# A hand-made instruction planner learns which work of VectorE and GpSimd to keep apart, the query tokens are put in order at their split, and the gates of the last token pair move forward

## The chip, the cores and the metric

The kernel runs on one core of one Trainium2 chip. The metric is the device time of one launch in microseconds. The runs of the kernel before gave 760.32, 760.10 and 758.83 us, median 760.1.

Five engines work side by side, each through its own queue in order: TensorE (PE; its weight loads are shown as PEld), VectorE (DVE), ScalarE (ACT), GpSimd (POOL) and SyncE (SP, which only issues DMAs). An instruction starts when those before it on its engine have been issued and the semaphores it waits for are set.

## The reference, cut to what matters

One pre-norm transformer block over 2 x 1024 tokens of width 1024 in float32:

```python
x = x + attn(layernorm(x))     # conv of width 3 (1024 -> 768), split in q, k, v of 256
                               # 16 heads of 64, causal softmax inside blocks of 128 tokens
                               # output product (1024 -> 256), then projection (256 -> 1024)
x = x + ffn(layernorm(x))      # y = x @ W_base.T + b_base
                               # + sum over 4 experts of alpha_e * 2 * (x @ A_e.T) @ B_e.T
                               # alpha = softmax(log(prior) + router logits of the 4 experts)
```

## The kernel before, in words

**Numbers.** Nearly every product is made of three float32r matmuls: each operand is split in a rounded part ("hi", a copy on ScalarE) and the rest ("lo", a subtraction on VectorE), and hi x hi, hi x lo and lo x hi are summed (`three`, L141). So each operand costs one ScalarE and one VectorE instruction.

**Three parts.** (1) To about 230 us: layernorm, transposes and the convolution, which is done with 6 products of transformed tokens and weights instead of 12; its results `m` go to DRAM. (2) About 230 to 520 us: attention. (3) From there: projection, second layernorm, and the feed-forward product by Strassen's scheme: for each pair `m` of 128-token groups, 7 products of 4x4 blocks take the place of 8. Sums of token blocks (S1 to S4) are made on the way; sums of weight blocks (T1 to T4, `plan_differences`) are made on GpSimd during attention (`stage_add`, L1080), split, and stored to DRAM (`wsd`).

**Attention.** 32 steps `i` (4 chunks of 512 tokens x 8 pairs of heads) are planned two at a time, 16 "pairs" `K`. For each step there are query and key products (`query_key`, out through ScalarE at L897), scores (`scores`, L905), mask (`masked`, VectorE, L920, reads PSUM), row maximum (`maximum`, VectorE, L929), exponentials with sums (`exponentials`, ScalarE, L934), reciprocal (`reciprocal`, VectorE, L941), the division (`normalized`, GpSimd, L945), transposes (L952) with copies out (`transposed_p`: half on VectorE at L960, half on ScalarE at L962), the product with the values (`attend`, L969), its split (L983, L990), and the output product (`out_proj`). Values are made for four heads at a time (`values`), and copied out by VectorE where `b` is odd (L871) and by ScalarE where it is even (L873).

**Tokens.** For the next chunk, the convolution's six results are loaded and joined on VectorE, all from SBUF: `tokens_join` in three parts (L560 and L561; L571, L572 and L573; L575 and L577), then split by `tokens_hi` (ScalarE, L585) and `tokens_lo` (VectorE, L590). Tiles 0 and 1 of a chunk feed the queries, 2 and 3 the keys, 4 and 5 the values. Tokens lie in the order (block, residue mod 4, position); the queries are brought into the order (block, position, residue) when they leave PSUM, by a strided write at L897.

**The planner.** The program's order isn't the source's order. Every piece of work is an `Op` with an engine, an assumed duration (`takes`), a due time, the earliest lead before it, the Ops it comes after with a `lag`, and places (buffers, PSUM banks) that it needs and gives. `trace()` plays the engines against each other in assumed time: again and again it takes, among all engines, the Op that can start earliest, preferring on each engine the first by due time that doesn't leave it idle. Then it emits all Ops sorted by their planned start. So assumed durations, lags and due times set nothing but the order in the queues; on the chip the semaphores of the data decide when a thing starts.

```python
t = [a.end + a.lag for a in self.after]
...
t = max(free.get(e, 0.0), o.due - o.lead + late, t)
```

**The last token pair.** In the loop over `m`, the small products for the gates (`z_products`, `plan_zs`), their turn (`z_turn`, in `plan_gate`), the gate's softmax (`gate_logits`, `gate_exp`, `gate`), a transpose (`transpose_z`, `plan_z`) and the four expert matmuls (`experts`, `plan_e`) come after product 5, 7 or 3 of the pair. In the pairs before the last, the next pair's projection and transposes lie between them. Each expert matmul adds into the PSUM bank of one quarter of the output (`py_a`, `py_e`, `py_f`, `py_c`), `add_y` (VectorE, L1376) adds that to the residual, and `store` writes it out, by halves in the last pair.

Of the kernel before, what the change touches and what calls it, by code (L numbers as in the profile page):

```python
# [21 lines left out]
P = 128  # L22
# [17 lines left out]
def preln_block_kernel(  # L40
# [229 lines left out]
    class Op:  # L270
        def __init__(self, engine, takes, due, lead, after, f, lag=0.15, need=(), give=()):
            self.engine, self.takes, self.due, self.lead = engine, takes, due, lead
            self.after, self.f, self.lag = [o for o in after if o is not None], f, lag
            self.need, self.give = need, give
            self.start = self.end = None
            plan.append(self)

        def earliest(self):
# [3 lines left out]
            t = [a.end + a.lag for a in self.after]  # L282
# [7 lines left out]
    def trace():  # L290
# [4 lines left out]
        while any(todo.values()):  # L295
            best = None
            for e, ops in todo.items():
                held = None
                for o in ops:
# [3 lines left out]
                    t = max(free.get(e, 0.0), o.due - o.lead + late, t)  # L303
                    if held is None or t < held[0]:
                        held = (t, o)
# [6 lines left out]
            free[o.engine] = o.end  # L312
            for k in o.need:
                places[k].remove(min(places[k]))
# [268 lines left out]
    def tokens_hi(ch, c):  # L583
        yt = t4(f"yt_{ch}_{c}", (2, TC))
        nc.scalar.copy(yt[:, 0], ys[ch, c])  # L585
        ys[ch, c] = ys[ch, c], yt

    def tokens_lo(ch, c):
        y, yt = ys[ch, c]
        nc.vector.tensor_tensor(yt[:, 1], y, yt[:, 0], ALU.subtract)  # L590
# [276 lines left out]
    def values_out(G, b):  # L867
        if G not in vhs:
            vhs[G] = ap_.tile([P, NB, 512], F32, tag="vh", name=f"vh_{G}")
        if b % 2:  # L870
# [17 lines left out]
    def query_key_out(i, q):  # L888
# [3 lines left out]
        out, pq = qk, pqs.pop((i, q))  # L892
        if q == 0:

            out = qk.rearrange("p (b j r) -> p b r j", b=NB, r=4)
            pq = pq.rearrange("p (b r j) -> p b r j", b=NB, r=4)
        nc.scalar.activation(out, pq, AF.Identity, bias=b_ap[:, hp : hp + 1], scale=sc)  # L897
# [374 lines left out]
    def z_products(m):  # L1272
# [13 lines left out]
        for o in ("A11", "A12", "S1"):  # L1286
            opd.pop((m, o))
# [101 lines left out]
    MM = 1.37  # L1389
    NI = NCHUNK * NHP  # L1390
# [13 lines left out]
    def op(key, e, takes, due, after, f, lead=14.0, **kw):  # L1404
        d[key] = Op(e, takes, due, lead, [d[a] for a in after if a in d], f, **kw)
        return d[key]

    def plan_q(i):
        ch, hp = divmod(i, NHP)
        for q in range(2):  # L1410
            pe(("Q", i, q), MM, [("y", ch, 2 * q), ("y", ch, 2 * q + 1)], partial(query_key, i, q),
               give=("t4",) * 2 if hp == NHP - 1 else ())
            op(("q", i, q), ACT, 0.55, at[0], [("Q", i, q)], partial(query_key_out, i, q),
               need=("t2",), give=("m",))

    def plan_v(G, b):
# [3 lines left out]
        op(("v", G, b), *((DVE, 0.6) if b % 2 else (ACT, 0.55)), at[0], [("V", G, b), ("v", G, 0)],  # L1420
           partial(values_out, G, b), need=("vh",) if b == 0 else (), give=("m",))

    def plan_s(i):
        pe(("S", i), 1.0, [("q", i, 0), ("q", i, 1)], partial(scores, i), need=("m",) * 2,
           give=("t2",) * 2)

    def plan_softmax(i, due):
        for j in range(2):
            op(("k", i, j), DVE, 0.69, min(due - 11.0, d["S", i].due + 4.0) + 0.7 * j, [("S", i), ("k", i, j - 1)],
               partial(masked, i, j), need=("a4",) if j == 0 else (), give=("m",), lead=40.0)  # L1430
        op(("x", i), DVE, 1.21, due - 9.5, [("k", i, 0), ("k", i, 1)], partial(maximum, i),
           lead=40.0)
        for j in range(2):
            op(("e", i, j), ACT, 1.6, due - 8.0 + 1.6 * j, [("x", i)], partial(exponentials, i, j),
               lead=40.0)
        op(("r", i), DVE, 0.2, due - 4.0, [("e", i, 0), ("e", i, 1)], partial(reciprocal, i),
           lead=40.0)
        op(("n", i), POOL, 2.3, due - 3.7, [("r", i)], partial(normalized, i), lead=40.0)

    def plan_t(i):  # L1440
        plan_softmax(i, at[0])
        for j in range(2):
            pe(("T", i, j), 0.44, [("n", i)], partial(transpose_p, i, j),
               give=("a4",) if j == 1 else ())
            op(("t", i, j), *((DVE, 0.65) if j == 0 else (ACT, 0.55)), at[0], [("T", i, j)],
               partial(transposed_p, i, j), need=("a4",) if j == 0 else (), give=("m",))

    def plan_o(i):
        pe(("O", i), 0.9, [("t", i, 0), ("t", i, 1)] + [("v", i // 4, b) for b in range(NB)],
           partial(attend, i), give=("a4",) + (("vh",) if i % 4 == 3 else ()))  # L1450
        op(("h", i), ACT, 0.6, at[0] + 1.0, [("O", i)], partial(attended_hi, i), need=("a4",))
        op(("l", i), DVE, 0.7, at[0] + 2.0, [("h", i)], partial(attended_lo, i), give=("m",))

    def plan_w(i):
# [3 lines left out]
        if hp == NHP - 1:  # L1458
            for wc in range(NWC):
                op(("oh", ch, wc), ACT, 0.7, at[0] + 1.0, [("W", i)], partial(out_hi, ch, wc),  # L1460
                   need=("t4",))
                op(("ol", ch, wc), DVE, 0.75, at[0] + 2.0, [("oh", ch, wc)],
# [5 lines left out]
    def plan_tokens(ch, c, due):  # L1468
# [3 lines left out]
        op(("yj", *k), DVE, 0.75, due - 5.0, [("yd", *k)], partial(tokens_join, ch, c, 0),  # L1472
           need=("t2", "t2"))
        op(("yk", *k), DVE, 1.0, due - 4.0, [("yj", *k)], partial(tokens_join, ch, c, 1))
        op(("yl", *k), DVE, 0.95, due - 3.0, [("yk", *k)], partial(tokens_join, ch, c, 2),
           give=("ml", "t2"))
        op(("yh", *k), ACT, 0.6, due - 1.8, [("yl", *k)], partial(tokens_hi, ch, c),
           need=("t4",))
        op(("y", *k), DVE, 0.64, due - 0.8, [("yh", *k)], partial(tokens_lo, ch, c),
           give=("t2",))  # L1480

    def plan_raw(k, src, due, hi, lo, pools, after=(), lead=8.0):
# [4 lines left out]
        op(("rh", *k), ACT, 0.58, due - 1.5, [("rd", *k), *after], partial(hi, *k[1:]), lead=lead)  # L1487
        op(("rl", *k), DVE, 0.66, due - 0.7, [("rh", *k)], partial(lo, *k[1:]), lead=lead,
           give=(pool,))

    def plan_x(n, due):
# [5 lines left out]
        op(("xb", n), POOL, 2.4, due - 4.0, [("X", n), ("pb",)], partial(add_projb, g))  # L1497

    def plan_p(n):
# [9 lines left out]
        for h in range(2):  # L1509
# [3 lines left out]
            op(("r", n, h, 0), DVE, 0.68, at[0] + 0.5, [("P", n, h), ("xb", n)],  # L1513
               partial(residual, g, h), give=("m",))
        op(("xs", n), DVE, 1.65, at[0] + 2.0, [("r", n, 0, 0), ("r", n, 1, 0)], partial(x_stats, g))
# [3 lines left out]
    def plan_tx(m, t, h):  # L1519
# [9 lines left out]
        if o == "A21":  # L1529
            more(("c", o), ACT, 0.6, 0.5, [("A", o)], partial(keep_a21, m), need=("a4",), give=("m",))  # L1530
        else:
            more(("h", o), ACT, 0.6, 0.5, [("A", o)], partial(op_hi, m, o), need=("a4",))
# [348 lines left out]
```

## Time and profile before

| what | us |
|---|---|
| profiled execution, device time | 760.05 |
| its span, first to last instruction | 758.3 |
| PE busy / idle in the span | 744.3 / 14.0 |
| DVE busy | 604.3 |
| ACT busy | 422.0 |
| POOL busy | 213.0 |
| `normalized` (L945), 32 times | 64.8 |
| queries out (L897, `bq`), 32 times | 38.0 |
| granted clock of TensorE (share) | 0.998 |

In a timeline, each line has the start and the duration in us, the engine, the line of the kernel, the operation, the tiles written and read, shapes, and how many were merged (x6). In brackets stands how long the engine was idle before it, and what ended that. A table of windows gives, for each stretch, its length and the busy time of PE, PEld, DVE, ACT and POOL with instruction counts, then TensorE's granted clock, the DMA engines' share and GB/s. Matmuls are pipelined: the durations of those that follow each other overlap a little, so the pace is read from the starts.

### The profile page before, as it was taken

How to read it: one execution, taken by the hardware profiler on the slowest of the kernel's cores; microseconds unless marked ns; L12 is line 12 of the kernel's file. 1: busy time of each engine (PE TensorE's matmuls, PEld its weight loads, DVE VectorE, ACT ScalarE, POOL GpSimd, SP SyncE). 2: the span in 40 equal slices, each digit the busy share in tenths (PEclk: the TensorE clock that was granted, in tenths of full speed). 3: DMA queues.
4: the chain of work that ended last, by engine and by line, in shares of the span. 5: the costliest groups of instructions: out<-in, count | busy, mean ns of one | idle time of the engine just before them, and what ended most of it. 6: DMA issues, size and time to landing. Idle time of an engine off the chain costs nothing.

```text
span 758.3 us, 12914 instructions
## 1 busy us (share of the span) xinstructions
PE 744.3 (98%) x4740; PEld 634.7 (84%) x4740; DVE 604.3 (80%) x1050; ACT 422.0 (56%) x1028; POOL 213.0 (28%) x170
## 2 busy tenths in 40 slices
PE   8999999999999999899999999999999999999997
PEld 8999988888888878787878888888888888888885
DVE  7888899889766899999899988789666767567652
ACT  6887336455736978797687989763212212212120
POOL 3224321210002224334332313362332241322410
PEclk9999999999999999999999999999999999999999
DMA  9937994994852323253316554795645565465552
GB/s 341 374 104 210 251 263 110 291 286 103 275 149 90 106 77 112 104 196 132 105 56 209 189 167 153 271 411 216 245 177 222 217 271 207 193 246 220 201 228 105
DMA packets 65279, 149.46 MB, mean 197 GB/s; under 512 B 5902, under 2 KB 24734, under 8 KB 60096
## 3 DMA queue, kind: packets, MB, share of 16 engines
q1 hardware_dynamic: 61488, 138.64, 50.6%
q0 software_dynamic: 3728, 10.00, 7.2%
q8 instruction: 37, 0.61, 0.3%
q14 instruction: 26, 0.21, 0.1%
HBM read 114.01 MB, written 34.60 MB: 196 GB/s over the span
## 4 chain that ended last, share of the span: by engine, by line
PE 82%; DVE 9%; ACT 6%; DMA 1%; issue 1%; SPq 0%; DVEq 0%; ACTq 0%
PE pm L141 26%; PE pq L141 8%; PE py_e L1262 6%; PE pp L141 6%; PE py_a L1262 6%; PE py_c L1262 6%; PE pw L141 4%; PE pv L141 4%; ACT p L934 3%; PE py_b L1262 3%; PE po L969 3%; PE pt L952 2%; PE s L905 2%; PE pz L1279 2%; PE trx L1202 2%; PE tr L386 1%
## 5 line engine op out<-in xcount | busy, mean ns | idle before, releaser
L141 PE MATMUL pm<-v,u 128*128 128x256 f32 (+1 forms) x1152 | 203.3, 337 | 1.1 <-ACT v L474 0.6
L141 PEld LDWEIGHTS pm<-v,u 128*128 128x128 f32 x1152 | 177.7, 190 | 24.3 <-ACT v L474 0.9
L934 ACT ACTIVATE p<-p,nmx 128x128 f32<-128x128 f32 x256 | 99.6, 397 | 12.8 <-DVE nmx L929 12.8
L945 POOL TENSOR_TENSOR p<-p,rs 128x1024 f32<-128x1024 f32 x32 | 64.8, 2025 | 144.8 <-DVE rs L941 120.3
L141 PE MATMUL pq<-yt,wqk 128*128 128x512 f32 x384 | 93.2, 397 | 0.0
L141 PEld LDWEIGHTS pq<-yt,wqk 128*128 128x128 f32 x384 | 70.7, 188 | 17.3 <-issue 1.9
L1165 POOL TENSOR_TENSOR xr<-xr,projb 128x1024 f32<-128x1024 f32 x16 | 38.3, 2398 | 96.7 <-DMA xr<-in_x 79.7
L934 ACT ACTIVATION_READ_ACCUMULATOR p<-p,nmx 128x1 f32 x256 | 50.1, 196 | 0.0
L920 DVE TENSOR_TENSOR p<-s,mask 128x512 f32<-128x512 f32 x64 | 42.2, 680 | 7.8 <-PE s L905 7.6
L141 PE MATMUL pw<-oT,wot 128*128 128x512 f32 x192 | 48.2, 398 | 0.0
L141 PE MATMUL pv<-wvt,yt 128*128 128x512 f32 x192 | 47.1, 395 | 0.0
L897 ACT ACTIVATE qk<-pq,bq 128x512 f32<-128x512 f32 x32 | 38.0, 1187 | 11.0 <-PE pq L141 8.2
L141 PEld LDWEIGHTS pv<-wvt,yt 128*128 128x128 f32 x192 | 36.0, 187 | 8.7
L141 PEld LDWEIGHTS pw<-oT,wot 128*128 128x128 f32 x192 | 35.9, 188 | 8.8 <-DVE oT L990 0.3
L424 POOL DMA_DIRECT2D g<-in_conv_w x24 | 21.2, 925 | 68.4 <-ACT g L420 36.6
L1240 ACT CAST S<-s 128x512 fp32r<-128x512 f32 x32 | 19.7, 621 | 35.8 <-DVE s L1234 31.5
L446 DVE TENSOR_TENSOR u<-g,u 128x768 fp32r<-128x768 f32 x40 | 37.5, 951 | 1.5 <-ACT u L442 1.4
L929 DVE TENSOR_REDUCE nmx<-p 128x8 f32<-128x1024 f32 x32 | 38.3, 1201 | 0.0
L905 PE MATMUL s<-qk,qk 64*128 64x128 f32 x512 | 34.6, 280 | 3.1 <-ACT vh L873 2.5
L905 PEld LDWEIGHTS s<-qk,qk 64*128 64x128 f32 x512 | 30.9, 187 | 7.6 <-ACT vh L873 3.2
L442 ACT CAST u<-g 128x768 fp32r<-128x768 f32 x40 | 32.5, 837 | 4.8 <-PE pm L141 4.7
L1360 ACT COPY u<-py_a 128x512 f32<-128x512 f32 x8 | 4.7, 588 | 53.0 <-PE py_a L1262 53.0
(204 smaller groups left out, 1539.9 us busy)
## 6 DMA issues: line engine op xcount, KB each, us to landing
wb_B<-wsd_B SPq DMA_DIRECT2D x32, 1024.0 KB, 4.8
g<-in_conv_w SPq DMA_DIRECT2D x48, 384.0 KB, 7.7
mdr<-m SPq DMA_DIRECT2D x36, 256.0 KB, 2.9
g<-in_conv_w POOLq DMA_DIRECT2D x24, 384.0 KB, 7.4
xt<-in_x SPq DMA_DIRECT2D x16, 512.0 KB, 9.5
xr<-in_x SPq DMA_DIRECT2D x16, 512.0 KB, 4.5
out<-xr SPq DMA_DIRECT2D x14, 512.0 KB, 2.9
ml<-mdr SPq DMA_DIRECT2D x18, 384.0 KB, 3.9
```

The costliest lines, as they stand in the source:

```text
L141: nc.tensor.matmul(ps, l[a], r[b], start=first and i == 0, stop=last and i == 2)
L442: nc.scalar.copy(us[v, dc][0], raws[v, dc])
L446: nc.vector.tensor_tensor(lo, raws.pop((v, dc)), hi, ALU.subtract)
L897: nc.scalar.activation(out, pq, AF.Identity, bias=b_ap[:, hp : hp + 1], scale=sc)
L905: nc.tensor.matmul(s[j][:, b, :], qh[ts(j, DH), ts(b, P)], kh[ts(j, DH), ts(b, P)], start=True, stop=True,)
L920: nc.vector.tensor_tensor(ps[i][0][:, ts(j, NB), :], ss[i][j], mask[:, None, :].to_broadcast([P, NB, P]), ALU.add,)
L929: nc.vector.tensor_reduce(nmx, p, AX.X, ALU.max, negate=True)
L934: nc.scalar.activation(p[:, k, :], p[:, k, :], AF.Exp, bias=nmx[:, k : k + 1], accum_out=sm[:, k : k + 1],)
L945: nc.gpsimd.tensor_tensor(p, p, rs[:, :, None].to_broadcast([P, 2 * NB, P]), ALU.mult)
L969: nc.tensor.matmul(po[ts(j, DH), ts(b, P)], vh[:, b, ds((i % 4) * P + j * DH, DH)], pT[:, j, ts(b, P)], start=True, stop=True,)
L1165: nc.gpsimd.tensor_tensor(xrs[g], xrs[g], pwt["b"], ALU.add)
L1262: nc.tensor.matmul(pys[m, b], l[x], r[y], start=opens and c == 0 and i == 0, stop=c == NH - 1 and i == 2, skip_group_check=not opens,)
```

## The change

It has five parts.

1. **The planner knows a port.** An Op may have `port=True`. Such an Op starts in the plan no earlier than the end of the last such Op on any engine. It is set for GpSimd's tensor work (`normalized`, `add_projb`, `stage_add`, `add_u`) and for VectorE's instructions with two tensor inputs in SBUF (`tokens_join`, `tokens_lo`, the "lo" of weights, stages and S sums, `za_lo`, `zd_lo`, `finish_bb`). It isn't set where an input is in PSUM, nor for `maximum`, `x_stats` and `x_norm`. This acts in the plan alone: no wait is added to the program.
2. **Assumed times.** Most `takes` are changed, by 0.03 to 0.4 us (`normalized` 2.3 to 1.9, masks 0.69 to 0.6, maximum 1.21 to 1.12). The default lag after VectorE and ScalarE goes from 0.15 to 0.25, between two Ops of TensorE to 0.
3. **Tokens and values.** The queries' tokens are written in their final order by `tokens_hi` and `tokens_lo` (tiles 0 and 1), and the strided write at L897 goes. `vh` is copied by VectorE for `b == 1` only.
4. **Stage work moves.** The differences start at the pairs 2, 4, 6, 8 instead of 1, 4, 6, 9 and have later due times within a pair; the splits of B11, B21 and B22 are spread over the pairs 10 to 14 instead of 11 to 14. Token tile 5 is planned ahead of others.
5. **The last pair** has its own order: gate products after product 1, gate in product 6, experts behind products 2, 3 and in the middle of 4, with stores of quarters between; the last expert matmul is ahead of the second half of product 4, and only its addition is left behind.

The diff, cut to its core (the many changed durations are left out):

```diff
-        def __init__(self, engine, takes, due, lead, after, f, lag=0.15, need=(), give=()):
+        def __init__(self, engine, takes, due, lead, after, f, lag=0.15, need=(), give=(), port=False):
...
+            self.port = port
...
-            t = [a.end + a.lag for a in self.after]
+            t = [a.end + (a.lag if a.engine != self.engine or a.engine != "PE" else 0.0)
+                 for a in self.after]
...
+                    if o.port:
+                        t = max(t, free.get("port", 0.0))
...
+            if o.port:
+                free["port"] = o.end
...
     def tokens_hi(ch, c):
         yt = t4(f"yt_{ch}_{c}", (2, TC))
-        nc.scalar.copy(yt[:, 0], ys[ch, c])
+        y, hi = ys[ch, c], yt[:, 0]
+        if c < NWC:
+
+            y = y.rearrange("p (b r j) -> p b r j", b=NB, r=4)
+            hi = hi.rearrange("p (b j r) -> p b r j", b=NB, r=4)
+        nc.scalar.copy(hi, y)
         ys[ch, c] = ys[ch, c], yt
...
-        nc.vector.tensor_tensor(yt[:, 1], y, yt[:, 0], ALU.subtract)
+        lo, hi = yt[:, 1], yt[:, 0]
+        if c < NWC:
+            y = y.rearrange("p (b r j) -> p b j r", b=NB, r=4)
+            lo, hi = (t.rearrange("p (b j r) -> p b j r", b=NB, r=4) for t in (lo, hi))
+        nc.vector.tensor_tensor(lo, y, hi, ALU.subtract)
...
-        if b % 2:
+        if b == 1:
             nc.vector.tensor_copy(vhs[G][:, b, :], pvs.pop((G, b)))
...
-        out, pq = qk, pqs.pop((i, q))
-        if q == 0:
-
-            out = qk.rearrange("p (b j r) -> p b r j", b=NB, r=4)
-            pq = pq.rearrange("p (b r j) -> p b r j", b=NB, r=4)
-        nc.scalar.activation(out, pq, AF.Identity, bias=b_ap[:, hp : hp + 1], scale=sc)
+        pq = pqs.pop((i, q))
+        nc.scalar.activation(qk, pq, AF.Identity, bias=b_ap[:, hp : hp + 1], scale=sc)
...
+        if e in (DVE, ACT):
+            kw.setdefault("lag", LAG)
...
-        op(("n", i), POOL, 2.3, due - 3.7, [("r", i)], partial(normalized, i), lead=40.0)
+        op(("n", i), POOL, 1.9, due - 3.7, [("r", i)], partial(normalized, i), lead=40.0, lag=0.3,
+           port=True)
...
-    DIFFERENCES = (1, 4, 6, 9)
+    DIFFERENCES = (2, 4, 6, 8)
     todo = [(n, c) for n in ("B11", "B21", "B22") for c in range(NH)]
-    SPLITS = {K: todo[3 * i : 3 * i + 3] for i, K in enumerate((11, 12, 13, 14))}
+    SPLITS = {10: todo[:2], 11: todo[2:5], 12: todo[5:7], 13: todo[7:10], 14: todo[10:]}
...
+    m = NM - 1
+    plan_product(m, 1)
+    plan_zs(m)
+    plan_product(m, 6, [partial(plan_gate, m)])
+    stream(m, "B21")
+    plan_product(m, 2)
+    plan_z(m)
+    plan_e(m, 0, 0, "a", [("Y", m, 2, 1)])
+    plan_store(m, 0, 0)
+    plan_product(m, 5)
+    stream(m, "B22")
+    plan_product(m, 7)
+    plan_product(m, 3)
+    plan_e(m, 0, 1, "e", [("Y", m, 3, 1)])
+    plan_store(m, 0, 1)
+    plan_e(m, 1, 1, "f", [], True)
+    plan_store(m, 1, 1)
+    plan_product(m, 4, [partial(plan_e, m, 1, 0, "c", [("Y", m, 4, 0)], sum_up=False)])
+    plan_add(m, 1, 0, "c", [("Y", m, 4, 1)])
+    plan_store(m, 1, 0)
```

## The prediction

> **What bounds the kernel now.** I read the page's busy shares first.
>
> ```profile
> PE 744.3 (98%) x4740; PEld 634.7 (84%) x4740; DVE 604.3 (80%) x1050; ACT 422.0 (56%) x1028; POOL 213.0 (28%) x170
> ```
>
> TensorE is busy 98% of the span and the change takes no matmul away. So the question is only where TensorE waits or lags, and which part of that can go. I looked at three stretches.
>
> (1) The timeline of PE in the attention part. One pair of head steps is always 24 `pq`, 12 `pw`, 12 `pv`, 16 `pt`, 32 `s` and 32 `po` matmuls, so the distance between the first `po` of one pair and of another measures the pace.
>
> ```profile
> 260.42 1.97 PE L969 MATMUL po<-pT,vh 128*64 128x128 f32 x32
> ...
> 437.69 1.97 PE L969 MATMUL po<-pT,vh 128*64 128x128 f32 x32
> ...
> 454.64 1.97 PE L969 MATMUL po<-pT,vh 128*64 128x128 f32 x32
> ...
> 471.58 1.97 PE L969 MATMUL po<-pT,vh 128*64 128x128 f32 x32
> ```
>
> The last two rows are one undisturbed pair: 471.58 - 454.64 = 16.94 us. From the first row to the second there are ten pairs: 177.27 us instead of 169.4. **The attention part loses 7.9 us**, all of it before 437.69. The wait table names what ends TensorE's waits there: mostly ScalarE's and VectorE's copies out of PSUM (`vh`, `pT`), which are late.
>
> (2) The windows table, by stage (PE, PEld, DVE, ACT, POOL busy).
>
> ```profile
> 262.30:318.40 56.10, 53.26 (x377) 43.90 (x375) 54.44 (x91) 45.13 (x147) 18.86 (x11) 1.00 0.30 97
> ...
> 439.60:473.50 33.90, 33.90 (x259) 28.67 (x257) 28.36 (x42) 30.83 (x97) 9.14 (x4) 1.00 0.49 167
> 519.50:728.30 208.80, 208.80 (x1148) 173.96 (x1147) 140.67 (x300) 42.06 (x83) 63.49 (x40) 1.00 0.56 215
> ```
>
> In 262 to 318 us, where three of those pairs lose most, VectorE is busy 54.44 of 56.10 us (97%). At 439 to 473 us, with VectorE at 84% and ScalarE at 91%, TensorE has no gap. So VectorE's share is the thing to explain. The last row is the feed-forward loop before its last pair: TensorE fills it wholly, and nothing can be won there.
>
> (3) The timeline at 302 us tells why VectorE is full.
>
> ```profile
> 302.11 2.15 POOL L945 TENSOR_TENSOR p<-p,rs 128x1024 f32<-128x1024 f32 x1 [2.15 <-DVE rs L941]
> ...
> 302.54 1.87 DVE L571 TENSOR_TENSOR y<-pq 128x128 f32<-128x128 f32 x1
> ...
> 304.22 1.33 POOL L1080 TENSOR_TENSOR pv<-pv_T,pv 128x512 f32<-128x512 f32 x1
> 304.33 1.38 DVE L572 SCALAR_TENSOR_TENSOR y<-pq 128x128 f32<-128x128 f32 x1
> 305.52 1.94 POOL L945 TENSOR_TENSOR p<-p,rs 128x1024 f32<-128x1024 f32 x1
> 305.63 1.98 DVE L573 SCALAR_TENSOR_TENSOR y<-pq 128x128 f32<-128x128 f32 x1
> 307.53 1.21 DVE L929 TENSOR_REDUCE nmx<-p 128x8 f32<-128x1024 f32 x1
> ...
> 308.77 0.40 ACT L934 ACTIVATE p<-p,nmx 128x128 f32<-128x128 f32 x1 [4.24 <-DVE nmx L929]
> ```
>
> Three additions that take 0.28 us elsewhere (L573: median 283 ns of 24) last 1.4 to 2.0 us, each ending just when the GpSimd instruction beside it ends. The maximum (L929) comes late, and ScalarE sits 4.24 us for it. Counted over 235 to 500 us of the trace: 29 of 180 VectorE instructions with both inputs in SBUF are at least 0.25 us above the shortest of their form, 37.6 us in all; of those with an input in PSUM (L920, 639 to 693 ns) none is. In 262 to 318 us this is 13.5 of the 54.4 us: without it VectorE would be busy 40.9 of 56.1 us, 73%.
>
> **The planner's change** (`port`, refitted durations, lag 0.25 for VectorE and ScalarE, none from PE to PE). It removes no instruction; it changes the order in which each engine gets them, so that two-input SBUF work and GpSimd's tensor work are not planned at the same time. No semaphore keeps them apart on the chip. Gain: between nothing and the 7.9 us of (1). With VectorE at 73% in the worst stretch, below the 84% that cost nothing at 439 us, I take 2.0 us of loss to remain for places where plan and chip drift apart: **-5.9 us**. The wait that is added is planned, not real: `normalized` (L945) is put behind token work. A token tile's four steps in the plan are 0.67 + 0.61 + 0.66 + 0.6 = 2.54 us. From the end of `normalized` to its first transpose the trace shows 1.0 to 17.6 us, in most of the 32 cases over 2.5, so most such delays are covered. Behind it on GpSimd stand the stage differences (L1080), which only the feed-forward weights wait for, tens of us later.
>
> The Trainium skill, "SBUF — State Buffer", section "SBUF: two separate sides", says that VectorE and GpSimd take a shared pair of ports as an exclusive lock for a whole instruction, that whichever starts first has it, and that VectorE's instructions in a 2-port mode need it too. By that rule GpSimd is blocked just as well, and the plan leaves `xn` (L1195), if that runs in such a mode, without the mark. The trace agrees: L945 takes 1896 to 3343 ns, and L1195 762 to 1924 ns with two long ones beside GpSimd work. By the rule those two stay long; in the sum this is nothing, since TensorE has no gap in that stage.
>
> **The queries' order at the split.** 32 strided query activations (L897 `bq`, 1.19 us) become plain ones (`bia`, 0.69): 32 x 0.50 = 16 us off ScalarE. Eight `tokens_hi` get the strided write: by the same two rows 8 x 0.5 = +4 us. Eight `tokens_lo` read with a stride on VectorE, which the trace doesn't show; from both sides: by L577, whose runs of 32 elements cost what L560's longer ones do (0.42 and 0.41 us for 256), nothing; by ScalarE's ratio 1.19/0.69, +0.5 us each, 4 us. L577 is the same engine and nearest: nothing. The copies of `vh` for b = 3 go to ScalarE: 8 x 0.57 = +4.6 us there, 8 x 0.68 = -5.4 us on VectorE. ScalarE nets -7.4 us over some 15 pairs. Beside TensorE these are no terms of the sum, they only let it keep its pace. The first chunk's split lies at 220 to 225 us, with 1.3 us of idle ScalarE after each copy, and the first query matmul at 230.1, so the 0.5 us are hidden.
>
> **Stage differences and splits moved.** They start a pair later, some 4 to 12 us later within it, and end a pair earlier (steps 2, 4, 6, 8 for 1, 4, 6, 9); the splits start one pair earlier. Each issue on SP goes along (loads 2.8 us to landing, stores 2.4 to 3.1). The last ones are still written before the loads of the feed-forward weights at the end of the attention part, and the DMA share there (0.79 to 0.93 at 473 to 519 us) doesn't rise: I cost it at nothing; if the cover were gone, product 1 at 519.6 us would start late by at most one landing, 3 us.
>
> **The last pair.** Now the chain at the end is in series: gate, transposes, four expert matmuls, four additions, stores.
>
> ```profile
> 751.23 0.28 PE L1343 MATMUL pzt<-identr,zr 128*98 128x128 f32 x2
> 751.61 0.37 ACT L1347 CAST zT<-pzt 98x256 fp32r<-98x256 f32 x1 [3.63 <-PE pzt L1343]
> ...
> 752.03 0.50 PE L1353 MATMUL py_a<-bb,zT 98*128 98x512 f32 x1 [0.52 <-ACT zT L1347]
> ...
> 752.57 0.69 DVE L1376 TENSOR_TENSOR xr<-py_a,xr 128x512 f32<-128x512 f32 x1 [3.13 <-PE py_a L1353]
> ...
> 754.37 0.68 DVE L1376 TENSOR_TENSOR xr<-py_c,xr 128x512 f32<-128x512 f32 x1
> ```
>
> The last addition ends at 755.05, the span 3.25 us later (store). In the new order the gate and all experts lie among the products, and one addition is left behind the last half of product 4. TensorE's work is the same: the chain has the transposes done at 751.53, the four experts take 4 x 0.23 = 0.93, so its last matmul would end at 752.46 without the 0.5 us wait; addition at 752.50 to 753.18. Gain 755.05 - 753.18 = **-1.9 us**. Moved earlier, the gate products need the split of A12, done by 725.6 against a start after 731; the loads of B22, 4.8 us to landing, are issued as product 2 frees its halves and have some 7 us (products 5 and 7 and the experts) to land. If one is late, some 1 us of the gain goes.
>
> **Sum.** Against the profiled execution's own 760.05 us (span 758.3 and 1.75 around it; the median of the runs is 760.1, so no correction): 760.05 - 5.9 - 1.9 = 752.25, and I say 752.4.
>
> **Rivals.**
> (A) Forecast, 750.2 (all 7.9 and 1.9 won) to 754.5: chance 0.62.
> (B) The order doesn't hold on the chip: nothing there waits for the port, and in-order queues drift against the plan, so about half of the long instructions come back. For it: GpSimd's starts hang on the reciprocals, which move with ScalarE. Against: after a reciprocal the plan puts work with PSUM inputs or the maximum, enough for 1.9 us. Loss 4 to 7.9: 756.1 to 760.05 - 1.9 = 758.2. Chance 0.20.
> (C) No change to be seen: half the attention loss stays and new waits cost what the tail gives; 758.5 to 761.6, chance 0.07.
> (D) Slower: `normalized` starts behind a whole token tile in every pair, 2.54 us late, and the transposes are late with it. With a slack of 1.0 to 1.5 us in each of 14 pairs this costs up to 14 x 1.3 = 18 us, less the gains, about 765. It decides from 7.8/14 = 0.56 us per pair. Against: slack is mostly 2.5 us and more. Chance 0.11.
>
> Within 0.2% (758.6 to 761.6) is about what a measurement of this kernel can't tell from no change. Faster: A + B = 0.82; same 0.07; slower 0.11. The range 750.2 to 758.2 covers A and B, 0.82.
>
> **What would show it.** Right: pairs from `po` to `po` near 16.94 us from 260 us on; L573, L577, L590 and L561 with maxima near their medians; VectorE at 75 to 80% in 262 to 318; L897 `bq` at 0.69 us; after the last `py_c` matmul one addition and one store. Wrong: long two-input instructions as before (B), or TensorE waiting at `pt` for GpSimd's `p` (D), or at the last pair's product 3 for `wb_B`.

## The result and the profile after

The changed kernel takes 767.62 us (median of 4 runs, 767.25 to 771.05), the kernel before 760.21 beside it: ratio 1.0111, interval 1.0079 to 1.0143. It is 7.4 us slower; the forecast was 7.7 us faster. The profiled execution took 767.25 us with a span of 765.4. Lines of the code stand some 12 higher than before (L945 is now L957, L1080 is L1092). First the busy shares on the page of the changed kernel.

```profile
PE 747.3 (98%) x4740; PEld 636.1 (83%) x4740; DVE 600.3 (78%) x1042; ACT 415.4 (54%) x1036; POOL 215.5 (28%) x170
```

The same 4740 matmuls, but TensorE is busy 3.0 us longer and idle 18.1 us instead of 14.0. Three landmarks place the 7.2 us of span: the first `pq` matmul starts at 229.74 (before: 230.13), the first `py_a` at 523.74 (519.57), and the span ends at 765.44 (758.27). So attention takes 294.0 us instead of 289.4 (**+4.6**), and from the first feed-forward product to the end it is 241.7 instead of 238.7 (**+3.0**). From the first `po` it now takes 180.6 us to do ten pairs; before it took 177.3.

The windows table of the changed kernel (columns: length, busy PE, PEld, DVE, ACT, POOL with counts, then TensorE's granted clock, DMA share, GB/s):

```profile
262.30:318.40 56.10, 53.58 (x395) 43.83 (x395) 49.26 (x90) 45.91 (x155) 22.25 (x12) 1.00 0.29 91
386.00:396.10 10.10, 7.54 (x51) 5.88 (x50) 10.10 (x13) 4.06 (x13) 5.11 (x3) 0.83 0.23 80
439.60:473.50 33.90, 33.90 (x254) 28.16 (x251) 26.53 (x45) 33.27 (x108) 8.47 (x4) 1.00 0.48 167
519.50:728.30 208.80, 208.80 (x1148) 174.26 (x1147) 145.23 (x301) 42.63 (x86) 65.90 (x41) 1.00 0.59 219
746.60:751.40 4.80, 4.80 (x15) 3.81 (x16) 0.69 (x1) 0.37 (x1) 0.00 (x0) 0.64 0.79 308
```

VectorE's share in the first stretch fell from 97% to 88%, and TensorE hardly gained (53.58 us for 53.26). New are the second and the last row: stretches in which TensorE waits, or gets a lower granted clock just after a wait (a mean of 0.83 and 0.64 in these rows).

**Where attention loses.** The timeline of the changed kernel at 251 to 260 us, VectorE, GpSimd and who waits:

```profile
251.11 3.76 POOL L957 TENSOR_TENSOR p<-p,rs 128x1024 f32<-128x1024 f32 x2 [10.29 <-DVE rs L953]
...
253.19 1.96 DVE L567 TENSOR_TENSOR pq<-ml 128x256 f32<-128x256 f32 x1
...
254.83 1.48 POOL L1092 TENSOR_TENSOR pv<-pv 128x512 f32<-128x512 f32 x1
...
255.07 1.52 DVE L568 TENSOR_TENSOR pq<-ml 128x256 f32<-128x256 f32 x1
...
256.39 1.33 POOL L1092 TENSOR_TENSOR pv<-pv_T,pv 128x512 f32<-128x512 f32 x1
256.51 2.06 DVE L606 TENSOR_TENSOR yt<-y,yt 128x512 fp32r<-128x512 f32 x1
...
258.67 0.69 ACT L909 ACTIVATE qk<-pq,bia 128x512 f32<-128x512 f32 x1 [2.56 <-DVE yt L606]
...
259.41 1.16 PE L917 MATMUL s<-qk,qk 64*128 64x128 f32 x16 [0.93 <-ACT qk L909]
```

GpSimd works almost without a break from 251.11 to 257.72, and three two-input instructions of VectorE, which by the port rule were not planned beside it, stand there. Each ends 0.3 to 0.9 us after the GpSimd instruction that it met: L567 0.28 us after the divisions at 254.87, L568 0.28 us after 256.31. ScalarE waits 2.56 us for the last of them, TensorE 0.93 us for ScalarE. Before, the stage differences (then L1080) ran at 236 to 240 us, ahead of the first division; now two of the three stand right behind the first two divisions. GpSimd's timeline of the kernel before:

```profile
236.26 1.30 POOL L1080 TENSOR_TENSOR pv_T<-pv_T,pv 128x512 f32<-128x512 f32 x1 [56.71 <-DMA pv<-in_w_base]
237.63 1.28 POOL L1080 TENSOR_TENSOR pv<-pv 128x512 f32<-128x512 f32 x1
239.00 1.27 POOL L1080 TENSOR_TENSOR pv<-pv_T,pv 128x512 f32<-128x512 f32 x1
250.18 1.90 POOL L945 TENSOR_TENSOR p<-p,rs 128x1024 f32<-128x1024 f32 x1 [9.92 <-DVE rs L941]
```

The same once more at 386 us, where the wait is longest:

```profile
386.21 1.90 POOL L957 TENSOR_TENSOR p<-p,rs 128x1024 f32<-128x1024 f32 x1 [1.47 <-DVE rs L953]
...
386.66 1.60 DVE L578 TENSOR_TENSOR y<-pq 128x128 f32<-128x128 f32 x1
...
388.07 1.35 POOL L1092 TENSOR_TENSOR pv<-pv_T,pv 128x512 f32<-128x512 f32 x1
388.18 1.39 DVE L579 SCALAR_TENSOR_TENSOR y<-pq 128x128 f32<-128x128 f32 x1
...
389.37 1.95 POOL L957 TENSOR_TENSOR p<-p,rs 128x1024 f32<-128x1024 f32 x1
389.49 1.98 DVE L580 SCALAR_TENSOR_TENSOR y<-pq 128x128 f32<-128x128 f32 x1
391.39 1.27 DVE L932 TENSOR_TENSOR p<-s,mask 128x512 f32<-128x512 f32 x2
392.12 1.18 PE L141 MATMUL pq<-yt,wqk 128*128 128x512 f32 x3 [2.56 <-DVE p L932]
```

Three joins of 0.28 us take 5.0 us together, the mask behind them is late, and TensorE waits 2.56 us for the mask. All of TensorE's gaps over 0.25 us in attention: 6.75 us after, 4.11 before. From 392.7 us on the granted clock is 0.50 for 3.4 us, which costs another 1.7 us. By the forecast's count (with the strided `tokens_lo` measured against its own shortest), held VectorE instructions fell only from 29 to 21, and their time from 37.6 to 24.2 us.

**Where the end loses.** The timeline of the changed kernel in the last pair:

```profile
742.52 1.29 POOL L1380 TENSOR_TENSOR xr<-xr,u 128x512 f32<-128x512 f32 x1 [23.23 <-DVE asum L1332]
742.68 1.15 DVE L1334 SCALAR_TENSOR_TENSOR a<-al,ar 128x8 f32<-128x8 f32 x1
...
743.77 2.34 POOL L1382 TENSOR_TENSOR xr<-xr,u 128x1024 f32<-128x1024 f32 x1
...
744.12 2.04 DVE L1347 CAST zr<-zs 128x64 fp32r<-128x64 f32 x1
...
746.58 0.34 PE L1355 MATMUL pzt<-identr,zr 128*98 128x128 f32 x2 [2.27 <-DVE zr L1349]
...
746.76 2.12 PE L1274 MATMUL py_e<-wb_wr,S 128*128 128x512 f32 x6
...
749.10 2.48 PE L1274 MATMUL py_e<-wb_wr,S 128*128 128x512 f32 x6
```

In its new place the gate's VectorE work meets the sums of `add_u` (L1380, L1382). A product with 8 columns takes 1.15 us (median of its 8 instances 168 ns), and a copy of 64 columns, which has one input, 2.04 us (median 196 ns); it ends 0.05 us after GpSimd does. TensorE waits 2.27 us for it, and the next groups of six matmuls take 2.12 and 2.48 us instead of 1.56, at a mean granted clock of 0.64. The plan marks none of the gate's VectorE work with `port`, so here it did not keep the two apart even on paper.

### The profile page after: what moved, and what is told of

Same layout as the page of the kernel before. It is cut to its first block, busy times and chain, and to the rows that moved or that the text cites. A ratio compares the mean times of both kernels' runs of the same rounds, so it can differ in the third digit from the quotient of the medians.

```text
span 765.4 us, 12872 instructions
## 1 busy us (share of the span) xinstructions
PE 747.3 (98%) x4740; PEld 636.1 (83%) x4740; DVE 600.3 (78%) x1042; ACT 415.4 (54%) x1036; POOL 215.5 (28%) x170
## 4 chain that ended last, share of the span: by engine, by line
PE 90%; DVE 6%; ACT 2%; DMA 1%; issue 0%; POOL 0%; ACTq 0%; DVEq 0%
PE pm L141 26%; PE pq L141 11%; PE py_c L1274 6%; PE py_e L1274 6%; PE pp L141 6%; PE pw L141 6%; PE py_a L1274 5%; PE pv L141 5%; PE po L981 3%; PE s L917 3%; PE pt L964 3%; PE py_b L1274 3%; PE pz L1291 2%; PE trx L1214 2%; PE tr L393 1%; ACT p L946 1%
## 5 line engine op out<-in xcount | busy, mean ns | idle before, releaser
L957 POOL TENSOR_TENSOR p<-p,rs 128x1024 f32<-128x1024 f32 x32 | 64.4, 2014 | 141.8 <-DVE rs L953 126.0
L141 PE MATMUL pq<-yt,wqk 128*128 128x512 f32 x384 | 95.5, 403 | 2.6 <-DVE p L932 2.6
L1236 ACT COPY s<-trx 128x512 f32<-128x512 f32 x8 | 4.7, 588 | 56.9 <-PE trx L1214 56.9
L981 PE MATMUL po<-pT,vh 128*64 128x128 f32 x512 | 32.4, 276 | 0.4 <-ACT pT L974 0.4
```

Of the source, the lines that this page charges most:

```text
L141: nc.tensor.matmul(ps, l[a], r[b], start=first and i == 0, stop=last and i == 2)
L957: nc.gpsimd.tensor_tensor(p, p, rs[:, :, None].to_broadcast([P, 2 * NB, P]), ALU.mult)
L981: nc.tensor.matmul(po[ts(j, DH), ts(b, P)], vh[:, b, ds((i % 4) * P + j * DH, DH)], pT[:, j, ts(b, P)], start=True, stop=True,)
```

## Theories and experiments

**Theory 1:** nothing on the chip keeps the planned separation, so VectorE is still held behind long GpSimd instructions, at other and worse places: beside the moved stage differences in attention, beside `add_u` in the last pair. **Theory 2 (rival):** the new order itself costs time, by port marks that make work late, or by the strided token instructions. Each run below is timed beside the kernel before (medians 759.85, 760.49, 760.07 and 759.94 us in the four groups, in the order used: last pair and short divisions; marks, stage, tokens, pieces; combinations, with e1b; single parts). Single executions of one kernel differ by up to 9 us, so the medians carry the verdicts and a single trace only the mechanism.

### Is it the long GpSimd instructions?

**e5_before_short** and **e6_after_short**: kernel before and changed kernel, the division cut from 1024 to 8 columns, so the rest of the probabilities stays undivided.

```diff
-        nc.gpsimd.tensor_tensor(p, p, rs[:, :, None].to_broadcast([P, 2 * NB, P]), ALU.mult)
+        nc.gpsimd.tensor_tensor(p[:, :, 0], p[:, :, 0], rs, ALU.mult)
```

> The kernel before, with the division of the probabilities on GpSimd cut to one column per block (8 instead of 1024 columns; the rest of the probabilities stays undivided). All queues keep their order. Theory 1 (GpSimd's long instructions hold VectorE, and this costs the attention part 7.9 us): some 2/3 of the held time goes (32 of 48 long GpSimd instructions there), 760.2 - 5 = 755 us. Rival (the attention part's loss is ScalarE's load or the order itself): 760 us, within 1 us.

> The changed kernel with the same cut of the division (8 of 1024 columns; the rest undivided), all queues in the changed order. Theory 1 (what the changed order loses in attention, some 12 us over an undisturbed pace, is again VectorE held by GpSimd): 767.6 - 9 = 758.6 us, and no wait over 0.5 us at 256 to 290 and at 392 us. Rival (the new order itself makes TensorE wait: buffers or copies are planned late): within 2 us of 767.6.

Measured: e5 753.0 us, 0.9910 [0.9892, 0.9928]; e6 758.05 us, 0.9989 [0.9974, 1.0004]. With short divisions attention takes 282.4 us in the old order (no gap) and 284.4 in the new (one gap, 0.38 us). So both kernels lose to the divisions: 7.0 us of 289.4 before, 9.6 of 294.0 after. But the medians of e5 and e6 are still 5.05 us apart, so only 2.4 of the 7.4 us between the two orders go with the divisions. In the traces 2.0 us are left in attention, of which one gap makes 0.38; and in e6 the wait for `zr` in the last pair is still 2.27 us, since `add_u` wasn't cut.

**e9_pieces**: the kernel before with the whole division, in four instructions of 256 columns.

```diff
+        for k in range(0, 2 * NB, 2):
-        nc.gpsimd.tensor_tensor(p, p, rs[:, :, None].to_broadcast([P, 2 * NB, P]), ALU.mult)
+            nc.gpsimd.tensor_tensor(p[:, k : k + 2, :], p[:, k : k + 2, :],
+                rs[:, k : k + 2, None].to_broadcast([P, 2, P]), ALU.mult)
```

> The kernel before with the division on GpSimd in 4 instructions of 256 columns instead of one of 1024; nothing left out, all queues in the old order. Theory 1 in its sharper form (VectorE waits only to the end of the one GpSimd instruction that runs): a held instruction costs at most some 0.6 us instead of 1.9, the attention part loses 2 to 4 us instead of 7.9: 755 to 757 us. Rival (the next piece takes the port again at once, so VectorE waits for all four, or the four instructions cost so much more on GpSimd that the transposes are late): 760 us or more.

Measured: **753.13 us, 0.9907 [0.9876, 0.9937]**, as fast as leaving the division out. Its timeline at the place that the forecast showed of before:

```profile
299.91 2.73 POOL L946 TENSOR_TENSOR p<-p,rs 128x256 f32<-128x256 f32 x4 [2.15 <-DVE rs L941]
...
300.34 0.58 DVE L571 TENSOR_TENSOR y<-pq 128x128 f32<-128x128 f32 x1
...
300.85 0.70 DVE L572 SCALAR_TENSOR_TENSOR y<-pq 128x128 f32<-128x128 f32 x1
...
301.47 0.70 DVE L573 SCALAR_TENSOR_TENSOR y<-pq 128x128 f32<-128x128 f32 x1
...
303.33 0.40 ACT L934 ACTIVATE p<-p,nmx 128x128 f32<-128x128 f32 x1 [0.43 <-DVE nmx L929]
```

The four pieces take 2.73 us instead of 1.90, but VectorE gets in between two of them: the three joins take 0.58 to 0.70 us instead of 1.38 to 1.98, and ScalarE waits 0.43 us for the maximum instead of 4.24. Over attention 50 instructions are held, for 21.9 us (before: 29, for 37.6), and TensorE has no gap over 0.25 us. The changed kernel's held time is not much more, 24.2 us, but in 21 holds, and its divisions cost it 9.6 us. The windows table of e9 corrects a reading in the forecast:

```profile
262.30:318.40 56.10, 56.05 (x405) 46.62 (x404) 54.20 (x103) 47.96 (x149) 25.23 (x32) 1.00 0.31 105
```

VectorE is again busy 97% of this stretch, and TensorE loses next to nothing (busy 56.05 of 56.10 us). So VectorE's share was not what cost; the length of a single hold fits all three kernels.

### Which part of the change costs what in attention?

**e17_plan_only**: the kernel before with the planner's change alone (parts 1 and 2, without the place of token tile 5).

```diff
+            self.port = port
+                    if o.port:
+                        t = max(t, free.get("port", 0.0))
+            if o.port:
+                free["port"] = o.end
...
-        op(("n", i), POOL, 2.3, due - 3.7, [("r", i)], partial(normalized, i), lead=40.0)
+        op(("n", i), POOL, 1.9, due - 3.7, [("r", i)], partial(normalized, i), lead=40.0, lag=0.3,
+           port=True)
```

> The kernel before with the planner's change alone: the port marks, the new durations and lags; tokens, values, stage work and the last pair as before. Theory (the separation exists only in the plan; on the chip long holds come back at other places): no gain. From the run with stage work as before and the mended last pair, 759.7, less that last pair's 1.7 (758.4 against 760.1), this gives some 761 us, with 24 to 40 us of VectorE's two-input time held. Rival (the planner's change wins what was forecast for it, and the stage work and the last pair hid that): 760.1 - 5.9 = 754.2 us, with TensorE's gaps in attention mostly gone.

Measured: 762.37 us, 1.0035 [1.0018, 1.0052], held 27.3 us. The part that was to bring 5.9 us costs 2.4. In its trace attention takes 291.0 us, 1.6 more than before; the first `pq` also starts late, at 231.98, but so it does in e1 (231.75), whose plan is the old one there. The trace has other gaps than before: 1.31 us at 349.66 and 0.76 at 368.24, for 1.52 at 312.48 and 1.01 at 384.14.

**e3_port_off**: the changed kernel, marks without effect, all else as changed.

```diff
-            self.port = port
+            self.port = False
```

> The changed kernel with the port flags without effect in the plan; refitted times, token order, moved stage work and the last pair's order stay. Theory 2 (the flags do their work on the chip in part: the time VectorE is held in attention fell from about 38 to 23 us with them, but where it is still held, TensorE has less slack): held time goes up again, above 30 us, and the time to 769 us or more. Rival A (the flags do harm, they bunch token work and GpSimd work into blocks that collide once the chip drifts from the plan): 763 to 766 us. Rival B (they do nothing that counts): 767 to 768 us.

Measured: 765.94 us, 1.0070 [1.0049, 1.0090]. Held time is 24.6 us without the marks and 24.2 with them: they separate next to nothing on the chip. The median is 1.7 us under the changed kernel's, at the upper edge of rival A's range, but the intervals of the two ratios overlap, so even this harm isn't sure. As the main cause the marks are out: without them the kernel is still 5.5 us slower than the one before.

**e4_stage_old**: the changed kernel, stage differences and splits at their old pairs and due times.

```diff
-    DIFFERENCES = (2, 4, 6, 8)
+    DIFFERENCES = (1, 4, 6, 9)
-    SPLITS = {10: todo[:2], 11: todo[2:5], 12: todo[5:7], 13: todo[7:10], 14: todo[10:]}
+    SPLITS = {K: todo[3 * i : 3 * i + 3] for i, K in enumerate((11, 12, 13, 14))}
...
-            op(("df", n, c), POOL, 1.38, due + (-2.0, -0.7, 4.0, 18.0)[i] + 4.0, after,
+            op(("df", n, c), POOL, 1.38, due + (-2.0, -0.7, 4.0, 10.0)[i], after,
```

> The changed kernel with the stage differences and splits at their old pairs (1, 4, 6, 9; 11 to 14) and old due times. Theory 2 (the first differences, now beside the first divisions at 251 to 258 us, start the early waits of 0.93, 0.74, 0.43, 1.16 and 0.94 us): these go or become less than half, 764 us. Rival (the early waits come from the token work alone): waits of 3 us or more in all stay between 250 and 290 us, 767 us.

Measured: 761.61 us, 1.0018 [0.9991, 1.0045], 6.0 less than the changed kernel. GpSimd's timeline in e4:

```profile
237.93 1.29 POOL L1092 TENSOR_TENSOR pv_T<-pv_T,pv 128x512 f32<-128x512 f32 x1 [56.94 <-DMA pv<-in_w_base]
239.31 1.28 POOL L1092 TENSOR_TENSOR pv<-pv 128x512 f32<-128x512 f32 x1
240.66 1.27 POOL L1092 TENSOR_TENSOR pv<-pv_T,pv 128x512 f32<-128x512 f32 x1
252.66 3.75 POOL L957 TENSOR_TENSOR p<-p,rs 128x1024 f32<-128x1024 f32 x2 [10.73 <-DVE rs L953]
```

The three differences are done by 242 us, and after the divisions GpSimd rests from 256.4 to 258.5. The token work meets less: L567 and L568 take 0.41 us each there, for 1.96 and 1.52 in the changed kernel.

**e15_differences_old** and **e16_splits_old** put back one each of what e4 puts back together: e15 the differences with all due times, e16 the pairs of the splits (`SPLITS`, as in e4's diff).

> The changed kernel with the stage differences at their old pairs and the old due times of differences and splits; only the pairs of the later splits are as changed. Theory (the loss comes from the first differences, which now run on GpSimd right behind the first divisions, where VectorE's token work is held): the early waits at 258 to 263 us go, and the time falls by 4 to 6 us, to 761.6 to 763.6. Rival (the loss comes from the splits that start a pair earlier): 767 us.

> The changed kernel with only the pairs of the later splits as before (11 to 14); differences and due times as changed. Theory (the first differences are the cost): nothing is won, 766 to 768.5 us, with the waits at 258 to 263 us still there. Rival (the splits are the cost): 761.5 to 763.5 us.

Measured: e15 764.01 us, 1.0050 [1.0031, 1.0068]; e16 768.52 us, 1.0120 [1.0095, 1.0145]. The differences are it (3.6 us, a little less than expected); the splits alone win nothing. That e4, with both, is another 2.4 us under e15 stays open; the intervals of the two overlap. The waits at 258 to 263 us are gone in e15's trace and there in e16's (0.67, 0.74 and 0.44 us).

**e7_tokens_old**: the changed kernel with the queries' tokens in the old order and the strided write at the query copies.

```diff
-        y, hi = ys[ch, c], yt[:, 0]
-        if c < NWC:
-            y = y.rearrange("p (b r j) -> p b r j", b=NB, r=4)
-            hi = hi.rearrange("p (b j r) -> p b r j", b=NB, r=4)
-        nc.scalar.copy(hi, y)
+        nc.scalar.copy(yt[:, 0], ys[ch, c])
...
+        out, pq = qk, pqs.pop((i, q))
+        if q == 0:
+            out = qk.rearrange("p (b j r) -> p b r j", b=NB, r=4)
```

> The changed kernel, same planned order in every queue, with the queries put in order where they were before (strided write at the query copies, plain tokens_hi and tokens_lo). VectorE's strided tokens_lo took 1.11 us instead of 0.68, 8 x 0.43 = 3.4 us; ScalarE's saving was 16 - 4 = 12 us. Theory 3 (the longer tokens_lo on VectorE helps to make the early waits): 1 us faster than the changed kernel, 766.6. Rival (ScalarE's saving counts, without it TensorE waits more): 769 us or more.

Measured: 768.55 us, 1.0099 [1.0069, 1.0128]. The new token order costs nothing; if anything it wins 0.9 us (the intervals overlap). That half of theory 2 is out too.

### The last pair

**e1_tail_only**: the kernel before with only the last pair's new order (part 5).

> The kernel before with the last pair's new order alone; attention is planned as before. Theory 1 (in the new last pair GpSimd's add_u holds VectorE's gate instructions, TensorE waits 2.3 us for the gate's transposes and then runs slow): the last pair costs 3.0 us as in the changed kernel, so 760.2 + 3.0 = 763.2 us. Rival (the last pair gains its 1.9 us as forecast, the whole loss comes from attention): 758.3 us.

Measured: 759.51 us, 0.9990 [0.9978, 1.0001], between the two and much nearer to the rival. The collision is there (L1310 1.15 us, L1322 1.69), but TensorE waits only 0.90 us for `zr`. From the first `py_a` to the end: 237.7 us, for 238.7 before.

**e2_gate_first**: the changed kernel; `u_second`, which feeds `add_u`, is planned behind the gate in the last pair. **e1b_tail_gate_first**: e1 with the same edit.

```diff
-            op(("u2", m), DVE, 0.6, at[0] + 0.5, [("Y", m, 6, 1), ("u1", m)], partial(u_second, m),
+            op(("u2", m), DVE, 0.6, at[0] + 0.5, [("Y", m, 6, 1), ("u1", m)]
+               + ([("g3", m)] if m == len(gs) // 2 - 1 else []), partial(u_second, m),
```

> The changed kernel, with one more dependence in the plan of the last pair: u_second comes after the gate on VectorE, so add_u on GpSimd can't start beside the gate. Theory 1: the casts and the small products of the gate take 0.2 us each again, the wait of 2.27 us at the transposes goes and the slow matmuls behind it (about 1.5 us) go too: 767.6 - 3.8 = 763.8 us. Rival (the gate is late for its own length, GpSimd only happens to run): no more than 0.5 us off, 767.1 us or more.

> The kernel before with the last pair's new order and the additions of V planned behind the gate; attention is as before. Theory (the gate's VectorE work held behind the additions of V took 0.4 to 0.9 us of what the last pair had to give): 760.2 - 1.4 to 1.9 = 758.3 to 758.8 us, no wait at the transposes of the gate, short casts there. Rival (that wait is hidden by what TensorE has to do anyway): 759.5 us, as without the second edit.

Measured: e2 766.02 us, 1.0076 [1.0048, 1.0104]; e1b **758.4 us, 0.9975 [0.9956, 0.9994]**. The last pair of e2:

```profile
745.13 0.20 DVE L1347 CAST zr<-zs 128x64 fp32r<-128x64 f32 x1
...
746.43 1.29 POOL L1380 TENSOR_TENSOR xr<-xr,u 128x512 f32<-128x512 f32 x1 [23.85 <-DVE u L1375]
...
747.45 0.28 PE L1355 MATMUL pzt<-identr,zr 128*98 128x128 f32 x2
747.57 1.62 PE L1274 MATMUL py_e<-wb_wr,S 128*128 128x512 f32 x6
```

The copy takes 0.20 us, GpSimd starts behind it, TensorE doesn't wait, and the groups of six take their normal time. From the first `py_a` to the end it is 237.2 us (changed kernel: 241.7). The whole of e2 won only 1.6 us, less than expected and with intervals that overlap: its attention took 296.0 us, 2.0 more, with a wait of 1.45 us at 320.13 and a granted clock of 0.50 for 3.4 us from 282.7 us on.

### Parts together

**e14_stage_old_gate_first**: the edits of e4 and e2 in one. **e12_after_pieces**: those of e9 and e2 on the changed kernel. **e13_best**: those of e9 and e1b on the kernel before.

> The changed kernel with two of its parts mended: stage differences and splits at their old pairs and due times, and the additions of V in the last pair planned behind the gate. Theory (the moved stage work costs some 6 us, the collision in the last pair 2 to 4.5 us, and the two add): 767.6 - 6.0 - 2 to 4.5 = 757.1 to 759.6 us, under the kernel before. Rival (they do not add: each edit moves the plan, and the holds come back at other places): 761 us or more.

> The changed kernel with the division in four GpSimd instructions of 256 columns and the additions of V in the last pair planned behind the gate. Theory (the order of the plan matters only through the long holds; with short pieces there is nothing left that a good or bad place can cost): as the kernel before with both edits, 751 to 753 us. Rival (the moved stage differences and the plan's separation cost something of their own, by GpSimd coming late, and the division planned at 1.9 us that takes some 2.7 makes that worse): 755 us or more, with TensorE waiting for the division or for copies out of PSUM behind it.

> The kernel before, with three edits: the division in four GpSimd instructions of 256 columns, the last pair in its new order, and the additions of V in the last pair planned behind the gate. Theory (the two losses are separate: VectorE held behind long GpSimd instructions in attention, worth 7.4 us to the kernel before; the gate and the additions of V colliding in the last pair, which without the collision ends 1.4 us sooner than the old last pair): 760.2 - 7.4 - 1.4 = 751.4 us. Rival (the last pair's gain is an accident of the late attention; what TensorE does not lose earlier, it waits for at the end): 753 us or more, as with the pieces alone.

Measured: e14 759.67 us, 0.9982 [0.9959, 1.0004]; e12 754.27 us, 0.9920 [0.9894, 0.9945]; **e13 751.87 us, 0.9887 [0.9850, 0.9923]**, the best of all. Its page:

```profile
PE 741.9 (99%) x4740; PEld 634.3 (85%) x4740; DVE 589.6 (79%) x1050; ACT 423.8 (57%) x1028; POOL 236.4 (32%) x266
```

GpSimd works 23.4 us more than before, and the span is 8.7 us shorter: TensorE has not one gap over 0.25 us from the first `pq` on. e14: the two mends add up almost as expected, but the result can't be told from the kernel before, while e1b can: what the changed kernel keeps besides (plan, durations, tokens) is worth no gain. e12 lies between theory and rival. No wait for the division shows up, so the rival's reason isn't seen; one wait of 0.60 us for a copy at 262.48 is left of the new order, and attention takes 284.6 us against 282.9 in e13. What makes up the rest of the 2.4 us between them stays open; it is about what e6 left in attention, too.

## Why the prediction was wrong, point by point

**What bounds the kernel: right.** Some 7 us of attention were there to be won, and by the cause that (3) named: e5 and e9 win 7 us with nothing done but shorter GpSimd instructions. The 7.9 us were a little too many: with no gap left (e5) the ten pairs take 170.3 us, not 169.4. Only the reasoning by VectorE's share in (2) was off, as e9's 97% shows.

**The step that failed: "-5.9 us" for the planner's change.** The forecast took a separation in the plan for one on the chip, with "2.0 us of loss to remain for places where plan and chip drift apart". The planner alone costs +2.4 us (e17), held time is 24 to 28 us with the marks or without (24.2 in the changed kernel, 24.6 in e3, 25.2 in e4, 27.3 in e17), and what remains sits elsewhere. The forecast had even written "No semaphore keeps them apart on the chip", and rival B for it, but B gave at worst the old loss of 7.9 us. That bound was wrong: a hold costs what the engines behind it lose, and a new order can put it where they have no slack.

**"I cost it at nothing" (stage work moved): wrong, some 3.6 us** (e15, with e16 as the control). The forecast followed the loads, the stores and the consumers, which were all in time; it did not ask what VectorE has to do beside a GpSimd instruction in its new place. In the kernel before, the first three differences ran ahead of the first division, at 236 to 240 us. The changed one put two of them right behind the first two, beside the next chunk's token work.

**"-1.9 us" for the last pair: the size right, the place not free.** Between the first `py_a` and the end, e1b takes 236.65 us, 2.05 less than before (by the medians it wins 1.7, its interval reaching from 0.5 to 3.3). In the changed kernel the same stretch is 3.0 longer: 2.27 us of wait for `zr` (the wait of before, 0.52, is gone), 0.50 x 3.4 = 1.7 us by the clock behind it, and a last store that takes 4.12 us from the end of the last addition to the end of the span, for 3.23 before (this is so in e6 and e7 as well, and not in the others; it stays open). The forecast followed TensorE, the split of A12 and the loads, and not which GpSimd work the gate would stand beside; nor did the marks cover the gate.

**The gate's copy.** The Trainium skill, "SBUF — State Buffer", section "SBUF: two separate sides", names VectorE's instructions in a 2-port mode among those that need the shared pair. The forecast used this for `xn` (L1195) and costed it at nothing; the gate's copy L1347, which the plan doesn't mark either, is the place where it counted: 0.196 us alone, 2.04 us beside GpSimd. The trace agrees with the rule in that the copy ends 0.05 us after the GpSimd instruction.

**The queries' order: nearly right.** L909 `bq` has a median of 684 ns (forecast 0.69). The strided `tokens_hi` takes 1.12 us for 0.62 (forecast +0.5). The strided `tokens_lo` takes 1.11 for 0.68: nearer to the upper bound than to the "nothing" taken, 8 x 0.43 = 3.4 us of VectorE. e7 shows that this decides nothing.

**Rivals and signs.** D did not happen: its waits for GpSimd's `p` come to one of 0.2 us, of a weight load. That D's 765 us lies near the measured time is chance. The loads of B22 were in time. Of the signs that were to show it right, the ten pairs from the first `po` on would have taken 169.4 us at 16.94 each and took 180.6, VectorE was at 88% in 262 to 318 us and not at 75 to 80, and L578, L580 and L606 reach 1.6, 2.0 and 2.4 us: the sign named for B.

## What to carry to other kernels

When two engines exclude each other on a resource, a plan that keeps them apart on paper helps only as far as the chip follows its times; make the excluding instruction short instead, so that the order counts for less (four pieces of 0.6 to 0.7 us in place of 1.9 won 0.9% here and cost GpSimd 24.5 us that nobody missed; the two orders were then 2.4 us apart instead of 7.4, with the gate planned ahead of `add_u` in both). When work is moved, look at what stands beside it on the other engine in its new place, small instructions included, not only at its data's path. And look at the longest single delay ahead of the bounding engine, not at the busy share of its suppliers.

## What the runs showed of the hardware that was not expected

**One GpSimd instruction is the unit of a hold.** VectorE gets its turn between two instructions of GpSimd that follow each other at once: at 300 us in e9 the three joins take 0.58 to 0.70 us beside pieces of 0.66 to 0.87, and 1.4 to 2.0 beside whole instructions.

**Short waits can cost TensorE its clock, but need not.** These are the two slow stretches of the changed kernel, in the windows table:

```profile
392.73:396.13 3.40, 3.40 (x10) 2.62 (x9) 3.40 (x5) 2.30 (x10) 0.00 (x0) 0.50 0.02 5
747.68:751.08 3.40, 3.40 (x10) 2.63 (x9) 0.69 (x1) 0.00 (x0) 0.00 (x0) 0.50 0.71 288
```

In the profiles of eight of these kernels there are 11 waits of 2.2 to 2.6 us. After 5 of them (both of the changed kernel, both of e7, one of two in e16) the granted clock was 0.50 for some 3.4 us, which cost the changed kernel 1.7 us each time; after the other 6 it stayed at 1.00. After two waits of about 1 us close together, at 280 us, it fell in the same way in e2, e7 and e16, and not in the changed kernel; in e3 it fell after a single wait of 1.36 us there. It is not an accident of the profiled execution: the mean granted clock was 0.991 to 0.995 in all four of the changed kernel, and 0.996 to 0.999 in the 18 of the kernel before beside e15. The Trainium skill, "TensorE: Matmul & The Clock Gate", section "Part 1: The HAM clock gate (the "warmup" mystery)", tells of half rate after an idle window of about 3.4 us, in a window that runs free of the program. The half rate and its 3.4 us agree with the trace, and that the outcome changes from run to run fits. But every wait here was shorter than 3.4 us, so a wait below that figure isn't safe.
